# Layer 1's output projection as seven block products, woven into the value products

## The chip, the cores and the metric

The kernel runs on one core of one Trainium2 chip. The metric is the device time of one execution in microseconds; all arithmetic is 32-bit floating point. The engines of the core are named here as the profile names them: PE (TensorE, the matrix engine; PEld is its weight load), DVE (VectorE), ACT (ScalarE), POOL (GpSimd) and SP (SyncE, which only issues DMAs). Each works through its own queue in order and waits for the others by semaphores.

## The reference

Two layers, each of the form `x = x + layer(group_norm(x))`, over x of shape 1 x 128 x 256 x 256 (128 rows of 256 positions with 256 channels). Layer 0 is attention along each row with 8 heads, a bias computed from a second input z, and a gate. The change is in layer 1 alone, banded attention with 4 heads:

```python
qkv = x2 @ w_in.T + b_in                      # x2: rows of 256 positions, 256 channels
q, k, v = jnp.split(qkv, 3, axis=-1)          # 4 heads of 64 channels
scores = jnp.einsum('bhid,bhjd->bhij', q, k) / sqrt(64)
scores = jnp.where(abs(i - j) <= 16, scores, -inf)
attn = softmax(scores)
out = jnp.einsum('bhij,bhjd->bhid', attn, v)
y = out @ w_out.T + b_out                     # the output projection
```

## The kernel before

Layer 0 takes the first 1980 us or so of the execution, layer 1 the rest. In layer 1 the 128 rows are worked on in 64 pairs (`Pair1`, `NP = 64`), and the order of all instructions is written out by hand (`tc.manual_schedule()`): what the loop `for p in range(NP - 1)` calls is queued on each engine in just that order. In loop pass p three pairs are in work. `now` (pair p) gets its scores and its first row's value sums, `was` (pair p - 1) its second row's value sums and its output projection, and `nxt` (pair p + 1) its q, k and v. Pair p + 2 (`nn`) is centred, and for pair p + 3 (`n3`) the loads are issued and, at the end of the pass, the transpose `turn()` (DVE).

The steps that the prediction follows:

- `product(n, i)` and `join(n, i)` (lines 1955 and 1989; n = 0, 1, 2 for q, k, v): the projection of a pair by w_in is two rows times two halves of the channels, a 2 x 2 block product, computed with seven products instead of eight. Products 1, 6, 7, 4 go one after the other into one PSUM bank (x), and after each one ACT copies the running sum out (into `u`, after product 4 to its place); products 2, 5, 3 go into the bank y, and after each one a `join` on DVE adds the copy in `u` to it. So product 6 adds onto x only when ACT has copied it, and product 5 overwrites y only when DVE has read it. The sums of blocks that these products need are made once for the weights (`mix_weights`, `wst`) and once per pair for the data (`differences`, `dT`, four POOL instructions). For q and k (line 1978) a product is one matrix product of 256 columns, for v (line 1974) it is two of 128 columns. Every 32-bit matrix product is two MATMUL records in the profile, each with its weight load.
- `scores(r)` (line 2031): 64 records on tiles of 64 x 64; then four exponentials on ACT (`e`) and four multiplications by the band `bw` on POOL (line 2042).
- `apply(r)` (lines 2056 and 2064): the value products on tiles of 64 x 32 into `o_eo`, and the row sums of `e` into `su_eo`. Then ACT copies one half of each (`copy_sums`, `copy_odd`), DVE adds the other half (`join_sums` line 2081, `join_odd` line 2084), inverts the sums (`invert`, line 2087) and multiplies (`weigh`, line 2092): `oT[r]`, the transposed result of row r.
- `out_row(r)` / `out_block(r, b)` (line 2110): the output projection, for each row and each half of its 256 positions two products of 256 columns into `su_y`. `keep_row(r)` (line 2118, DVE) adds `xt` (the layer's input plus the output's bias, which `add_bias`, line 1933, adds on POOL) and writes `yo`; after row 1 SP stores it.
- `some_checks(n)` runs up to n entries of a list of range checks on DVE (lines 2143 to 2146), which feed a verdict at the end; for the last 8 pairs (`LATE`) there are more of them. What is left of the list is run after the loop.

`su_y` is one tile over two PSUM banks: the row sums lie in the first half of each bank, the output projection's result in the second halves.

Of the kernel before, what the change touches and what calls it, by code (L numbers as in the profile page):

```python
# [9 lines left out]
F32 = mybir.dt.float32  # L10
# [6 lines left out]
P = 128  # L17
# [756 lines left out]
def fast_kernel(  # L774
# [1057 lines left out]
    with tc.tile_pool(name="l1", bufs=2) as sb, tc.tile_pool(  # L1832
# [14 lines left out]
        for sign, base in ((1, 0), (-1, GE - 1)):  # L1847
# [2 lines left out]
                base=base, pattern=[[sign * P, KC], [-sign * GE, G]], channel_multiplier=sign,  # L1850
            )
        wst = sb.tile([P, 4, 3, P], F32, name="wst", bufs=1)

        def norm1():

# [29 lines left out]
        def mix_weights():  # L1885

            a = [[w_in[:, k].rearrange("p (n m c) -> p m n c", n=3, m=KC)[:, m] for k in range(KC)]
                 for m in range(KC)]
            s1, s2, s3, s4 = (wst[:, n] for n in range(4))
            nc.gpsimd.tensor_tensor(s1, a[1][0], a[1][1], ALU.add)  # L1890
            nc.gpsimd.tensor_tensor(s2, s1, a[0][0], ALU.subtract)
            nc.gpsimd.tensor_tensor(s3, a[0][0], a[1][0], ALU.subtract)
            nc.gpsimd.tensor_tensor(s4, a[0][1], s2, ALU.subtract)


        o_eo = [ps_o.tile([P, 2, I], F32, name=f"ps_o1_{n}", tag=f"o{n}") for n in range(2)]
        su_y = ps_o.tile([P, 2, 2, I], F32, name="ps_su_y1", tag="su")
        su_eo = [su_y[:, n, 0] for n in range(2)]

        class Pair1:  # L1900

# [52 lines left out]
            def product(self, n, i):  # L1954

                if len(self.ps) == n:
                    self.ps.append([mm1("ps_qk", n % 2) for _ in range(2)])
                    self.u.append(sm.tile([P, 3, I], F32, name="u1", tag=f"u{n}", bufs=2))
# [12 lines left out]
                if n == 2:  # L1971
                    for b in range(NB):
                        at = slice(b * P, (b + 1) * P)
                        nc.tensor.matmul(  # L1974
                            to[:, at], rhs[:, at], lhs, start=start and b == 0, stop=True, skip_group_check=True
                        )
                else:
                    nc.tensor.matmul(to, lhs, rhs, start=start, stop=True, skip_group_check=True)  # L1978
                u = self.u[n]
                if i in (2, 5, 3):  # L1980
                    return
                at = (1, 6, 7, 4).index(i)
                to = self.to[n](1, 0) if i == 4 else u[:, at]
                if n == 2:
                    nc.scalar.copy(to, x.rearrange("p (b c) -> p b c", b=NB) if i == 4 else x)
                else:
                    nc.scalar.activation(to, x, AF.Identity, bias=bin_c[:, n * KC + (at > 1) : n * KC + (at > 1) + 1])  # L1987
# [59 lines left out]
            def apply(self, r):  # L2047


                e = self.es[r]  # L2050
                gap = q0(2) - q0(0)
                for a in range(2):
                    for j in range(NK // 2):
                        for h in range(H1):
                            for k in (2 * j, 2 * j + 1):
                                nc.tensor.matmul(  # L2056
                                    o_eo[k % 2][h * DH : (h + 1) * DH, a, q0(k) : q0(k) + W],
                                    self.v[half(k), r, j, h * D1 + a * DH : h * D1 + (a + 1) * DH],
                                    e[half(k), h % 2, h // 2, j * W : (j + 1) * W], start=True, stop=True,
                                )  # L2060
                for h in range(H1):
                    for n in range(2):
                        two = su_y[h * DH : (h + 1) * DH, n].rearrange("p a i -> p (a i)")
# [39 lines left out]

            def out_block(self, r, b):
                if b == 0:
                    self.y = su_y[:, :, 1]
                    if self.p == NP - 1:
                        self.y = mm1("ps_y1", r).rearrange("p (b c) -> p b c", b=NB)
                for k in range(KC):
                    nc.tensor.matmul(  # L2110
                        self.y[:, b], self.oT[r][:, k, b * P : (b + 1) * P], w_out[:, k, :],
                        start=(k == 0), stop=(k == KC - 1),
                    )

            def keep_row(self, r):
                if r == 0:
                    self.yo = sb.tile([P, 2 * NB, C], F32, name="yo", tag="yo")
                nc.vector.tensor_tensor(
                    self.yo[:, r * NB : (r + 1) * NB, :], self.y,
                    self.xt[:, r * NB : (r + 1) * NB, :], ALU.add,  # L2120
                )
# [44 lines left out]
        with tc.manual_schedule():  # L2166
# [3 lines left out]
            mix_weights()  # L2170
            for k in range(KC):
                now.centre(k)
            for t in (*o_eo, su_y):
                nc.vector.memset(t, 0.0)
            nxt.turn()
            for m in range(KC):
# [8 lines left out]
            look_all(eb.rearrange("p h b i -> p (h b i)"), math.exp(-20.0))  # L2185
            n_eb = cols[0]

            was = Nobody()
            for p in range(NP - 1):
                nn = pair1(p + 2) if p == 0 else n3  # L2190
                n3 = pair1(p + 3)
# [10 lines left out]

                now.scores(0)
                now.scores(1)
                was.apply(1)
                nxt.begin_fast()
                was.copy_sums(1)
# [4 lines left out]
                for n in range(2):  # L2212
                    nxt.product(n, 2)
                    nxt.join(n, 2)
                was.invert(1)
                some_checks(p > 0)
                for i in (6, 5, 7):
                    for n in range(2):
                        nxt.product(n, i)
                for n in range(2):  # L2220
                    nxt.join(n, 5)
                was.join_odd(1)
                was.weigh(1)
                was.out_row(0)
                for n in range(2):
                    nxt.product(n, 4)
                    nxt.product(n, 3)
                    nxt.join(n, 3)
                fast = p < NP - 2
                if fast:  # L2230
                    nxt.product(2, 1)
                    nxt.product(2, 2)
                    nxt.join(2, 2)
                nn.centre(0)
                some_checks(2 if p > NP - LATE else 0)

                now.apply(0)
                now.copy_sums(0)
                if fast:
                    nxt.product(2, 6)  # L2240
                    nxt.product(2, 5)
                now.copy_odd(0)
                now.join_sums(0)
                was.out_block(1, 0)
                if fast:
                    nxt.product(2, 7)
                now.join_odd(0)
                some_checks(2 if p > NP - LATE else p > 0)
                was.out_block(1, 1)
                if fast:  # L2250
                    nxt.join(2, 5)
                was.keep_row(1)
                if fast:
                    nxt.product(2, 4)
                    nxt.product(2, 3)
                    nxt.join(2, 3)
                now.invert(0)
                now.weigh(0)
                nn.centre(1)
                nn.differences()  # L2260
                nn.add_bias()
                n3.turn()
# [3 lines left out]
                was, now, nxt = now, nxt, nn  # L2266

            now.scores(0)
            was.apply(1)
            was.copy_sums(1)  # L2270
            was.copy_odd(1)
# [104 lines left out]
```

## Time and profile before

| what | value |
|---|---|
| median of 3 runs | 3122.07 us (3119.59 to 3122.21) |
| the profiled execution | 3124.98 us |
| its span in the profile | 3123.2 us |
| mean granted PE clock | 0.987 |
| mean of L1974, 128-column products (first form) | 284 ns |
| mean of L1978, 256-column products (dT, wst) | 379 ns |
| mean of L2110, output projection in the loop | 386 ns |
| mean of L2092, `weigh` | 944 ns in the loop |
| mean of L1933, bias on POOL | 2383 ns |

A line L1974 is line 1974 of the kernel before. The mean of a matrix product is from its start to its modelled end; products overlap, so what one costs in a run of them is the distance from one start to the next, which is read from the chain or the timeline and is shorter. An engine's busy share is over the whole span, both layers together. "PE 100%" says that PE always has a product in flight, not that it is at its peak.

### The profile page before, as it was taken

Reading aid. Unit: us, or ns where it says so; the run is one execution under the profiler, and the core shown is the slowest. Engines: PE = TensorE matmul, PEld = TensorE weight load, DVE = VectorE, ACT = ScalarE, POOL = GpSimd, SP = SyncE. Lnnn points to the kernel's source line nnn. Section 1 sums busy time; section 2 is a strip of 40 time slices with the busy share of each in tenths; the row PEclk is TensorE's granted clock in tenths of the full one; section 3 lists DMA queues with packets and bytes.
Section 4 is the critical chain, followed back from the end, with each engine's and each line's share of the span. In section 5 each row is a group of like instructions: output and inputs, shape, how many; then the busy total and the mean of one; then the engine's idle time right before and its main releaser. Section 6 shows DMA issues by size and latency. Waiting matters only on the chain.

```text
span 3123.2 us, 80605 instructions
## 1 busy us (share of the span) xinstructions
PE 3020.6 (97%) x33642; PEld 2102.9 (67%) x33642; DVE 2397.7 (77%) x4010; ACT 1574.3 (50%) x2639; POOL 2267.1 (73%) x1636
## 2 busy tenths in 40 slices
PE   5689999999999999999999999899999999999998
PEld 4355555565555556555555655688888888888887
DVE  7986677777777777777777777688878777777788
ACT  3454544444444444444444444355555555555553
POOL 3469889888889989888998987454555555555553
PEclk9799999999999999999999999999999999999999
DMA  9952323323332332333233232443434343444431
GB/s 359 390 181 52 99 69 99 99 64 93 94 99 69 100 99 64 90 97 99 69 99 99 64 89 75 118 104 83 103 84 98 90 98 89 95 92 95 92 95 51
DMA packets 690774, 327.90 MB, mean 105 GB/s; under 512 B 538624, under 2 KB 639872, under 8 KB 689248
## 3 DMA queue, kind: packets, MB, share of 16 engines
q1 hardware_dynamic: 686000, 320.02, 38.3%
q8 instruction: 266, 4.36, 0.6%
q10 hardware_dynamic: 4400, 2.63, 0.3%
q14 instruction: 108, 0.88, 0.1%
HBM read 253.83 MB, written 68.74 MB: 103 GB/s over the span
## 4 chain that ended last, share of the span: by engine, by line
PE 92%; DMA 3%; DVE 3%; ACT 1%; POOL 1%; issue 1%; ACTq 0%; SPq 0%; POOLq 0%; DVEq 0%
PE ps_p L1364 21%; PE ps_qk L1978 12%; PE ps_sc L1401 9%; PE ps_ov L1436 8%; PE ps_y L1490 7%; PE ps_su_y L2110 7%; PE ps_qk L1974 7%; PE ps_v L1382 7%; PE ps_o L2056 4%; PE ps_su L1444 3%; PE ps_sc L2031 3%; PE ps_su_y L2064 2%; DMA xa<-in_x_dram 2%; DVE st L1199 1%; DMA zt<-in_z_dram 1%; PE ps_t L1143 1%
## 5 line engine op out<-in xcount | busy, mean ns | idle before, releaser
L1425 POOL TENSOR_TENSOR eboth<-e 128x512 f32<-128x512 f32 x512 | 743.4, 1473 | 178.3 <-PE ps_su L1444 98.4
L1421 DVE TENSOR_TENSOR e<-ps_sc,eb 128x1024 f32<-128x1024 f32 x384 | 458.5, 1222 | 292.3 <-ACT ps_sc L1413 292.2
L1413 ACT ACTIVATE ps_sc<-ps_sc 128x1024 f32<-128x1024 f32 x384 | 375.4, 1007 | 438.8 <-PE ps_sc L1401 313.1
L1401 PE MATMUL ps_sc<-qT,kT 32*128 32x256 f32 x4096 | 293.9, 400 | 0.0
L1941 POOL TENSOR_TENSOR dT<-xgT,dT 128x256 f32<-128x256 f32 x63 | 45.9, 728 | 313.7 <-ACT xgT L1927 313.7
L2042 POOL TENSOR_TENSOR e<-e,bw 128x384 f32<-128x384 f32 x256 | 248.1, 1000 | 10.7 <-ACT e L2040 10.7
L2110 PE MATMUL ps_su_y<-w_out,oT 128*128 128x256 f32 x1008 | 254.5, 386 | 0.9 <-DVE sums L2081 0.9
L1490 PEld LDWEIGHTS ps_y<-wo,oT 128*128 128x128 f32 x1024 | 195.5, 191 | 86.9 <-issue 44.2
L1401 PEld LDWEIGHTS ps_sc<-qT,kT 32*128 32x128 f32 x4096 | 185.5, 184 | 101.7 <-issue 91.3
L1490 PE MATMUL ps_y<-wo,oT 128*128 128x256 f32 x1024 | 244.7, 382 | 5.8 <-POOL oT L1480 5.8
L1436 PE MATMUL ps_ov<-e,v 128*32 128x256 f32 x4096 | 248.6, 383 | 0.0
L1364 PE MATMUL ps_p<-xnT,wq 128*128 128x512 f32 x512 | 247.6, 606 | 0.1
L1364 PE MATMUL ps_p<-xgT,wg 128*128 128x512 f32 x512 | 247.3, 605 | 0.0
L1382 PE MATMUL ps_v<-wv,xnT 128*128 128x256 f32 x1024 | 241.9, 379 | 0.0
L1364 PE MATMUL ps_p<-xnT,wk 128*128 128x512 f32 x512 | 240.7, 592 | 0.0
L1382 PEld LDWEIGHTS ps_v<-wv,xnT 128*128 128x128 f32 x1024 | 194.7, 190 | 53.8 <-issue 30.9
L2087 DVE RECIPROCAL rv<-sums 128x256 f32<-128x256 f32 x128 | 223.1, 1743 | 0.0
L1987 ACT ACTIVATE u<-ps_qk,bin_c 128x256 f32<-128x256 f32 x378 | 174.4, 475 | 95.0 <-PE ps_qk L1978 95.0
L2110 PEld LDWEIGHTS ps_su_y<-w_out,oT 128*128 128x128 f32 x1008 | 181.9, 190 | 22.2 <-DVE sums L2081 1.3
L1436 PEld LDWEIGHTS ps_ov<-e,v 128*32 128x32 f32 x4096 | 120.5, 110 | 109.0 <-issue 42.5
L1364 PEld LDWEIGHTS ps_p<-xnT,wk 128*128 128x128 f32 x512 | 97.3, 190 | 122.7 <-issue 122.5
L1940 POOL TENSOR_TENSOR dT<-xgT 128x256 f32<-128x256 f32 x63 | 46.0, 730 | 183.6 <-ACT xgT L1927 183.6
(234 smaller groups left out, 6608.5 us busy)
## 6 DMA issues: line engine op xcount, KB each, us to landing
xa<-in_x_dram SPq DMA_DIRECT2D x8, 4096.0 KB
xt<-in_x_dram SPq DMA_DIRECT2D x64, 512.0 KB
x<-xo SPq DMA_DIRECT2D x16, 2048.0 KB
xt<-x SPq DMA_DIRECT2D x64, 512.0 KB
rvb<-rsum SPq DMA_DIRECT2D x252, 128.0 KB
xs<-x SPq DMA_DIRECT2D x252, 128.0 KB
out_dram<-yo SPq DMA_DIRECT2D x63, 512.0 KB
xs<-in_x_dram SPq DMA_DIRECT2D x248, 128.0 KB
```

The source lines that it names most:

```text
L1364: nc.tensor.matmul(ps, w[:, k, m * P : (m + 1) * P], getattr(self, src)[:, k, :], start=(k == 0), stop=(k == KC - 1),)
L1382: nc.tensor.matmul(self.ps_v[:, b * C : (b + 1) * C], self.xnT[:, k, t * P : (t + 1) * P], wv[:, k, :], start=(k == 0), stop=(k == KC - 1),)
L1401: nc.tensor.matmul(self.pss[q // 2][:, q % 2, b, :], self.kT[rs, c, r * I + b * P : r * I + (b + 1) * P], self.qT[rs, c, r * I : (r + 1) * I],
L1413: nc.scalar.activation(self.pss[a], ps, AF.Exp)
L1421: nc.vector.tensor_tensor(es[a], pss[a], eb[:, h : h + 2], ALU.mult)
L1425: nc.gpsimd.tensor_tensor(t, es[a][:, :, 0, :], es[a][:, :, 1, :], ALU.add)
L1436: nc.tensor.matmul(ov[q * D0 : (q + 1) * D0, c, :], self.v[:, r, b, h * D0 : (h + 1) * D0], es[q // 2][:, q % 2, b, :], start=(b == 0), st ...
L1490: nc.tensor.matmul(self.ps_y[:, b * C : (b + 1) * C], self.oT[r][:, k, b * P : (b + 1) * P], wo[:, k, :], start=(k == 0), stop=(k == KC - 1),)
L1978: nc.tensor.matmul(to, lhs, rhs, start=start, stop=True, skip_group_check=True)
L2042: nc.gpsimd.tensor_tensor(e[:, q], e[:, q], bcast(bw.rearrange("p b w -> p (b w)"), 1, KC), ALU.mult)
L2087: nc.vector.reciprocal(self.rv[:, r, :], self.sums)
L2110: nc.tensor.matmul(self.y[:, b], self.oT[r][:, k, b * P : (b + 1) * P], w_out[:, k, :], start=(k == 0), stop=(k == KC - 1),)
```

## The change

The output projection of the pairs of loop passes 1 to 62 is computed by the same seven-product scheme over the pair's two rows: `out_product(i)` with 128-column products in place of `out_row`. The last two pairs, after the loop, keep the old form. `su_y` becomes two tiles, one per bank; the second half of bank 0 is x of the scheme, that of bank 1 is y. The sums of blocks of w_out are four POOL instructions in `mix_weights` (`wso`), those of the data four POOL instructions per pair (`row_sums`, `oS`). ACT copies after products 1, 6, 7, 4, DVE joins after 2, 5, 3. The input and bias are added by one POOL instruction per pair in the next pass (`keep_rows`), which also issues the store.

The order in the pass changes with it. `apply(0)` moves ahead of the last two products (4 and 3) of q and k; `join_odd(1)` ahead of the reciprocal; behind q's and k's last products come 14 steps in which the value products of `nxt` and the output products of `was` take turns. The transpose `turn()` of n3 moves into that run, and of the range checks in the late passes there are four entries instead of five. The buffer `u` has one copy instead of two. In `after`, the line numbers are some 7 higher up to `apply`; the new products are at line 2156, their copies at 2162 and 2164, the joins at 2169, `row_sums` at 2129 to 2132, `keep_rows` at 2172.

```diff
+        wso = sb.tile([P, 4, P], F32, name="wso", bufs=1)
...
+            a = [[w_out[:, k, m * P : (m + 1) * P] for k in range(KC)] for m in range(KC)]
+            s1, s2, s3, s4 = (wso[:, n] for n in range(4))
+            nc.gpsimd.tensor_tensor(s1, a[1][0], a[1][1], ALU.add)
+            nc.gpsimd.tensor_tensor(s2, s1, a[0][0], ALU.subtract)
+            nc.gpsimd.tensor_tensor(s3, a[0][0], a[1][0], ALU.subtract)
+            nc.gpsimd.tensor_tensor(s4, a[0][1], s2, ALU.subtract)
...
-        su_y = ps_o.tile([P, 2, 2, I], F32, name="ps_su_y1", tag="su")
-        su_eo = [su_y[:, n, 0] for n in range(2)]
+        su_y = [ps_o.tile([P, 2, I], F32, name=f"ps_su_y{n}", tag=f"su{n}") for n in range(2)]
+        su_eo = [t[:, 0] for t in su_y]
...
+            def row_sums(self):
+                self.oS = sb.tile([P, 4, I], F32, name="oS1", tag="oS", bufs=1)
+                b = [[self.oT[r][:, k, :] for r in range(2)] for k in range(KC)]
+                t1, t2, t3, t4 = (self.oS[:, n] for n in range(4))
+                nc.gpsimd.tensor_tensor(t1, b[0][1], b[0][0], ALU.subtract)
+                nc.gpsimd.tensor_tensor(t2, b[1][1], t1, ALU.subtract)
+                nc.gpsimd.tensor_tensor(t3, b[1][1], b[0][1], ALU.subtract)
+                nc.gpsimd.tensor_tensor(t4, b[1][0], t2, ALU.subtract)
...
+            def out_product(self, i):
...
+                x, y = (t[:, 1] for t in su_y)
+                w = lambda m, k: w_out[:, k, m * P : (m + 1) * P]
+                b = lambda k, r: self.oT[r][:, k, :]
+                to, rhs, lhs, start = {
+                    1: (x, w(0, 0), b(0, 0), True),
+                    2: (y, w(0, 1), b(1, 0), True),
+                    6: (x, wso[:, 1], self.oS[:, 1], False),
+                    5: (y, wso[:, 0], self.oS[:, 0], True),
+                    7: (x, wso[:, 2], self.oS[:, 2], False),
+                    4: (x, w(1, 1), self.oS[:, 3], False),
+                    3: (y, wso[:, 3], b(1, 1), False),
+                }[i]
+                for n in range(NB):
+                    at = slice(n * P, (n + 1) * P)
+                    nc.tensor.matmul(
+                        to[:, at], lhs[:, at], rhs, start=start and n == 0, stop=True, skip_group_check=True
+                    )
+                if i in (2, 5, 3):
+                    return
+                if i == 4:
+                    nc.scalar.copy(self.quarter(1, 0), x.rearrange("p (b c) -> p b c", b=NB))
+                else:
+                    nc.scalar.copy(self.uy[:, (1, 6, 7).index(i)], x)
...
+            def out_join(self, i):
+                m, r, at = {2: (0, 0, 0), 5: (1, 1, 2), 3: (0, 1, 1)}[i]
+                y, u = (t.rearrange("p (b c) -> p b c", b=NB) for t in (su_y[1][:, 1], self.uy[:, at]))
+                nc.vector.tensor_tensor(self.quarter(m, r), y, u, ALU.add)
...
+            def keep_rows(self):
+                nc.gpsimd.tensor_tensor(self.yo, self.yo, self.xt, ALU.add)
+                nc.sync.dma_start(rows(out, 2 * self.p, 2), self.yo)
...
                 now.scores(1)
+                old.keep_rows()
                 was.apply(1)
...
+                was.join_odd(1)
                 was.invert(1)
-                some_checks(p > 0)
                 for i in (6, 5, 7):
                     for n in range(2):
                         nxt.product(n, i)
+                nn.centre(0)
+
+                now.apply(0)
+                now.copy_sums(0)
                 for n in range(2):
                     nxt.join(n, 5)
-                was.join_odd(1)
                 was.weigh(1)
-                was.out_row(0)
+                was.row_sums()
+                some_checks(2 if p > NP - LATE else p > 0)
+                now.join_sums(0)
                 for n in range(2):
                     nxt.product(n, 4)
+                now.copy_odd(0)
+                for n in range(2):
                     nxt.product(n, 3)
                     nxt.join(n, 3)
+                now.join_odd(0)
                 fast = p < NP - 2
                 if fast:
                     nxt.product(2, 1)
                     nxt.product(2, 2)
                     nxt.join(2, 2)
...
+                nn.centre(1)
+                nn.differences()
+                nn.add_bias()
+                was.out_product(1)
+                was.out_product(2)
+                was.out_join(2)
                 if fast:
                     nxt.product(2, 6)
                     nxt.product(2, 5)
...
-                was.out_block(1, 0)
+                was.out_product(6)
                 if fast:
                     nxt.product(2, 7)
...
-                was.out_block(1, 1)
+                n3.turn()
+                was.out_product(5)
+                was.out_product(7)
                 if fast:
                     nxt.join(2, 5)
-                was.keep_row(1)
+                    nxt.product(2, 4)
+                some_checks(2 if p > NP - LATE else p > 0)
+                was.out_join(5)
                 if fast:
-                    nxt.product(2, 4)
                     nxt.product(2, 3)
                     nxt.join(2, 3)
+                was.out_product(4)
+                was.out_product(3)
+                was.out_join(3)
                 now.invert(0)
                 now.weigh(0)
```

More of the change, by code (lines that the diff above doesn't have):

```diff
@@ L1957, in product @@
                     self.ps.append([mm1("ps_qk", n % 2) for _ in range(2)])
-                    self.u.append(sm.tile([P, 3, I], F32, name="u1", tag=f"u{n}", bufs=2))
+                    self.u.append(sm.tile([P, 3, I], F32, name="u1", tag=f"u{n}", bufs=1))
                 x, y = (ps[:, :I] for ps in self.ps[n])
@@ L2062, in apply @@
                     for n in range(2):
-                        two = su_y[h * DH : (h + 1) * DH, n].rearrange("p a i -> p (a i)")
+                        two = su_y[n][h * DH : (h + 1) * DH].rearrange("p a i -> p (a i)")
                         nc.tensor.matmul(
@@ L2105, in out_block @@
                 if b == 0:
-                    self.y = su_y[:, :, 1]
+                    self.y = [t[:, 1] for t in su_y]
                     if self.p == NP - 1:
-                        self.y = mm1("ps_y1", r).rearrange("p (b c) -> p b c", b=NB)
+                        ps = mm1("ps_y1", r)
+                        self.y = [ps[:, n * C : (n + 1) * C] for n in range(NB)]
+                        self.whole = ps
                 for k in range(KC):
                     nc.tensor.matmul(
-                        self.y[:, b], self.oT[r][:, k, b * P : (b + 1) * P], w_out[:, k, :],
+                        self.y[b], self.oT[r][:, k, b * P : (b + 1) * P], w_out[:, k, :],
@@ new lines, in quarter @@
+            def quarter(self, m, r):
+                return self.yo[:, r * NB : (r + 1) * NB, m * P : (m + 1) * P]
+            def out_product(self, i):
+                if i == 1:
+                    self.yo = sb.tile([P, 2 * NB, C], F32, name="yo", tag="yo")
+                    self.uy = sm.tile([P, 3, I], F32, name="uy1", tag="uy", bufs=1)
+                x, y = (t[:, 1] for t in su_y)
[21 more added lines that the diff above has]
+                    nc.scalar.copy(self.uy[:, (1, 6, 7).index(i)], x)
@@ L2117, in keep_row @@
                     self.yo = sb.tile([P, 2 * NB, C], F32, name="yo", tag="yo")
[L2118 to L2121, printed above, removed]
+                if self.p == NP - 1:
+                    nc.vector.tensor_tensor(
+                        self.yo[:, r * NB : (r + 1) * NB, :], self.whole.rearrange("p (b c) -> p b c", b=NB),
+                        self.xt[:, r * NB : (r + 1) * NB, :], ALU.add,
+                    )
+                for t in range(r * NB, (r + 1) * NB if self.p < NP - 1 else 0):
+                    nc.vector.tensor_tensor(self.yo[:, t, :], self.y[t - r * NB], self.xt[:, t, :], ALU.add)
                 s0 = 2 * self.p
@@ L2172, in fast_kernel @@
                 now.centre(k)
-            for t in (*o_eo, su_y):
+            for t in (*o_eo, *su_y):
                 nc.vector.memset(t, 0.0)
@@ L2186, in fast_kernel @@
             n_eb = cols[0]
-            was = Nobody()
+            old = was = Nobody()
             for p in range(NP - 1):
@@ L2233, in fast_kernel @@
                     nxt.join(2, 2)
[L2234 to L2238, printed above, removed]
+                nn.centre(1)
[4 more added lines that the diff above has]
+                was.out_join(2)
                 if fast:
@@ L2241, in fast_kernel @@
                     nxt.product(2, 5)
-                now.copy_odd(0)
-                now.join_sums(0)
-                was.out_block(1, 0)
+                was.out_product(6)
                 if fast:
                     nxt.product(2, 7)
-                now.join_odd(0)
-                some_checks(2 if p > NP - LATE else p > 0)
-                was.out_block(1, 1)
+                n3.turn()
+                was.out_product(5)
+                was.out_product(7)
                 if fast:
                     nxt.join(2, 5)
-                was.keep_row(1)
+                    nxt.product(2, 4)
+                some_checks(2 if p > NP - LATE else p > 0)
+                was.out_join(5)
                 if fast:
-                    nxt.product(2, 4)
                     nxt.product(2, 3)
                     nxt.join(2, 3)
+                was.out_product(4)
+                was.out_product(3)
+                was.out_join(3)
                 now.invert(0)
                 now.weigh(0)
[L2259 to L2262, printed above, removed]
                 if p == NP // 2:
@@ L2265, in fast_kernel @@
                     below(n_eb, n_mask, 1e15)
-                was, now, nxt = now, nxt, nn
+                old, was, now, nxt = was, now, nxt, nn
             now.scores(0)
+            old.keep_rows()
             was.apply(1)
```

## The prediction

> **What bounds the kernel now.** The profiled execution took 3124.98 us, its span 3123.2 us; the median of the three timed runs is 3122.07. I carry the sum as a difference, so it applies to either. The page comes first: its busy table and the by-engine line of the chain that ended last.
>
> ```profile
> PE 3020.6 (97%) x33642; PEld 2102.9 (67%) x33642; DVE 2397.7 (77%) x4010; ACT 1574.3 (50%) x2639; POOL 2267.1 (73%) x1636
> PE 92%; DMA 3%; DVE 3%; ACT 1%; POOL 1%; issue 1%; ACTq 0%; SPq 0%; POOLq 0%; DVEq 0%
> ```
>
> Busy shares are averages over two layers, so the second view is the windows by stage. In layer 1's loop:
>
> ```profile
> 2600.00:2700.00 100.00, 100.00 (x1755) 86.88 (x1756) 76.47 (x114) 57.42 (x129) 55.02 (x52) 1.00 0.41 92
> ```
>
> The columns are TensorE, weight loads, VectorE, ScalarE, GpSimd, granted clock, DMA share, GB/s. TensorE is never idle, the clock is full, GpSimd is at 55%: only TensorE time per loop pass counts. The third view, the chain in order of time over one pass, gives it piece by piece (start, us, what):
>
> ```profile
> 2590.92 4.51 PE ps_qk L1978 x20
> 2595.43 1.73 PE ps_su_y L2110 x8
> 2597.16 1.73 PE ps_qk L1978 x8
> 2598.88 1.09 PE ps_qk L1974 x8
> ...
> 2601.26 1.09 PE ps_qk L1974 x8
> 2602.35 0.96 PE ps_su_y L2110 x4
> 2603.31 0.44 PE ps_qk L1974 x4
> 2603.76 0.87 PE ps_su_y L2110 x4
> 2604.62 0.89 PE ps_qk L1974 x8
> 2605.51 1.48 PE ps_sc L2031 x64
> ```
>
> The next pass's first product piece starts at 2608.28, so a pass is 17.36 us. Each matrix product is two records. A 256-column record costs 1.73/8 = 0.216 us, a 128-column one 0.89/8 = 0.111. Four pieces cost more than that: both long x8 pieces of L1974 (1.09, 0.20 over), the first row-1 block of L2110 (0.96, 0.10 over) and the first L1978 piece (4.51 against 20 x 0.216 = 4.33, 0.18 over). The fourth view, line L1974 by source, shows what such an excess is:
>
> ```profile
> L1974 PE MATMUL ps_qk<-wst,dT x744: 272/275/378, 2008.6 to 3075.4; 128*128 128x128 f32 x186
>   issue: 18.9, 62
> ```
>
> Minimum, median and maximum are 272, 275 and 378 ns: where a product's first weight load could not start ahead, about 0.10 us of it lies open. The 18.9 us of idle time before line L1974, 62 times 0.30, are the change from the small tiles of `apply` to full tiles, once per pass.
>
> **Part by part: TensorE.** Removed per pass: two `out_row`s, 16 records of 256 columns, 16 x 0.216 = 3.46 us. Added: seven products of two blocks, 28 records of 128 columns, 28 x 0.111 = 3.11. Difference -0.35. Three excesses move. (1) Value product 2 now waits for VectorE's q join 3, which the timeline shows ending at 2616.17 + 0.41 = 2616.58 while that product's group has been running since 2616.09: 0.10 wait and 0.10 open load. In the new order q's product 3, k's product 3 and value product 1 lie in front of it, and no `keep_row` on VectorE: -0.20 if the join is in time. (2) The 0.10 in front of the first row-1 block was its wait for `join_sums` (the block starts at 2602.19, VectorE's `sums` ends at 2601.70 + 0.42 = 2602.12; `su_y` is one tile); split in two and moved far behind that join: -0.10. (3) The 0.20 behind `apply(0)` stays, now before an L1978 product, 0.18 as behind `apply(1)`: -0.02. Together -0.67.
>
> A rule speaks against the 128-column form: the Trainium skill, "TensorE: Matmul & The Clock Gate", section "The mechanism" of Part 3, says that a weight load overlaps running matmuls only when its row group differs, and its section "LDWEIGHTS" gives columns / 1.2 GHz, 107 ns for 128. Were every load in the open, 28 x 0.107 against 16 x 0.107 would cost 1.28 us more a pass; with the -0.35 that is +0.93, a loss of 57 us over 61 passes. The row answers it: value products of this very shape, one load each, run at 0.111 us.
>
> **Does anything else become late?** The run of 18 steps alternates value and output products at 4 x 0.111 = 0.445 us each. On the x bank each next product waits for a ScalarE copy of the last (1, 6, 7, 4); on the y bank each waits for a VectorE join (2, 5, 3). The price of one hop is in the timeline:
>
> ```profile
> 2603.15 0.61 PE L1974 MATMUL ps_qk<-wst,dT 128*128 128x128 f32 x4
> 2603.80 0.37 ACT L1985 COPY u<-ps_qk 128x256 f32<-128x256 f32 x1 [0.99 <-PE ps_qk L1974]
> ```
>
> 0.61 from first start to last end, 0.04 to ScalarE, 0.37 copy, about 0.05 back, and the weight load wants to begin 0.11 ahead: 1.18 us from product to dependent product. Value 6 to 7, 7 to 4, output 6 to 7, 7 to 4 are each three products apart, 1.33: 0.15 to spare. Product 3 waits for a join that needs the copy of 7: 1.18 + 0.04 + 0.42 = 1.64 against four products, 1.78: 0.14 to spare, for values and outputs. Value 2: 0.59 (two 256-column records) + 0.04 + 0.42 + 0.05 + 0.11 = 1.21 against 0.43 + 0.43 + 0.445 = 1.31: 0.10. So seven of the fourteen products are tight by 0.10 to 0.15, the other seven have 0.3 or more. I allow 0.05 per pass (from 0, if all are in time, to 1.4, if all seven miss as value 2 does now at 0.20 each). Term: -0.62.
>
> ScalarE gains four copies of 0.37, 1.5 us on 57% of 17.4: 11.4 of 16.75. VectorE loses two `keep_row`s (0.68 each) and gains three joins (0.42): even, 13.3 (76.5%) of 16.75, and it is a queue in order: join 3 and both `out_join`s stand behind checks (0.3 to 0.7 us) in the first 25 passes or so (some 50 entries, two a pass), inside the 0.05.
>
> GpSimd carries the most:
>
> ```profile
> 2607.71 1.25 POOL L1943 TENSOR_TENSOR dT<-xgT,dT 128x256 f32<-128x256 f32 x1
> 2608.92 2.36 POOL L1933 TENSOR_TENSOR xt<-xt,bout_r 128x1024 f32<-128x1024 f32 x1
> 2611.24 3.86 POOL L2042 TENSOR_TENSOR e<-e,bw 128x384 f32<-128x384 f32 x4
> ```
>
> Now 3 x 0.73 + 1.25 + 2.36 + 3.86 = 9.7; `keep_rows` adds one 128x1024 op (2.36), `row_sums` four of 128x256 (2.9 to 3.4, as dT's): 15.0 to 15.5 of 16.75. Laid out from the start of `scores(0)`: masks 1.5 to 5.4, `keep_rows` to 7.8, then it waits for `weigh(1)` (VectorE: `sums` 3.5, two joins, `join_odd`, reciprocal 5.9 to 7.6, two joins, `weigh` 8.4 to 9.1), `row_sums` to 12.0 or 12.5, differences to 15.9, bias to 18.3 = 1.5 of the next pass. Its customers are later: `apply(0)` at 7.2 needs masks done at 3.5; output 6 at 13.0 needs the second sum, at 10.6; the next pass's product 6 at 4.6 needs differences done before that pass began. Cover 3.7, 2.4 and over 4 us; without it every us late would stand on the path. `weigh(1)` takes 1.25 where a mask runs beside it instead of 0.69 (2614.40, L2092); here it meets `keep_rows` or nothing, at most 0.8 by that line's maximum of 1.48, which the 2.4 covers.
>
> SyncE: the out DMA moves from the pass's end to behind `keep_rows` (7.8), the sums' DMA behind `weigh(1)` (9.1), the next loads behind both. Loads now start at 2605.81 and the transpose that reads their kind runs a pass later, about 20 us; 9.1 of one pass to 12.8 of the next (the transpose's new place) is the same 20. Nothing.
>
> Once only. First pass: `apply(0)` comes before values, at 1999.68 + 4.4 = 2004.1, but GpSimd's two bias ops (1999.40, 4.68) put the masks at 2004.1 to 2006.0: +1.9. Last loop pass: no value products to alternate with, the copy chain 3 x 1.18 + 2 x 0.445 = 4.4 against 3.56 now: +0.9. Tail: one check entry fewer per late pass puts eight more check instructions (0.28 to 0.42, some 2.4 us) before the last `keep_row`s, where VectorE idles 0.73: +1.7. The four `wso` ops lie in GpSimd's idle 5.4 us before 1995.43: nothing. Sum +4.5.
>
> 61 passes x -0.62 = -37.8; +4.5; -33.3 us. 3122.07 - 33.3 = 3088.8, for the profiled execution 3091.7.
>
> **Rivals.** *Part of it is lost:* one or two of the seven tight waits miss each pass, 0.20 each as value 2 misses now. -0.67 + 0.40 = -0.27, x 61 + 4.5 = -12: 3110 at two. For it: spare of 0.10 to 0.15 is smaller than the scatter VectorE's checks and `weigh` bring; passes of 17.6 to 18.4 us between score groups occur now. Against: the two joins and copies nearest in kind in today's value products do keep time.
> *Slower, by open weight loads:* the run turns into a chain of hops, product 4 and 7 of both kinds and both 3s late. Six x 0.20 = 1.2 - 0.67 = +0.53, x 61 + 4.5 = +37: 3159. It decides from the fourth late product per pass (three give 3122 + 0). Against it: a miss pushes the later products back and so gives the next hop its spare.
> *GpSimd becomes the bound* and holds the masks or sums: it needs its pass above 16.75, that is each op 8% dearer or one more collision of 0.5 on two ops, and above 17.4 to lose; 3.7 us of cover must go first. At 18.0: +0.6 x 61 = 3163.
> *Nothing changes:* three misses a pass.
>
> **How the numbers follow.** Forecast (up to half a miss) 0.60; part lost 0.25; nothing 0.03; slower by open loads 0.08; GpSimd 0.04. A measurement of this kernel tells about 0.2%, 6 us, from no change: faster 0.85, same 0.03, slower 0.12. The range's low end takes -0.76 a pass (the 128-column record before `apply` costs 0.09 more than others, and that place falls to a 256-column one): -46 + 4 = 3080, rounded to 3078; its high end is two misses, 3110.
>
> **What would show it.** Right: passes of 16.7 to 16.8 us between score groups; 28 records of the new line at 275 ns median, few at 378; GpSimd near 90%, TensorE 100%. Wrong: TensorE waits on ScalarE or VectorE inside the run, `apply(0)` waiting for GpSimd, passes above 17.

## The result: slower, and where it happens

The change takes 3168.47 us (median of 4 runs, 3165.91 to 3174.12) against 3122.01 for the kernel before on the same chip: ratio 1.0152, 95% interval 1.014 to 1.0164. The profiled execution took 3166.87 us, its span 3165.1. The page shows the kind of loss at once (busy table; the chain that ended last, by engine):

```profile
PE 3008.4 (95%) x34386; PEld 2100.6 (66%) x34386; DVE 2427.1 (77%) x4075; ACT 1656.9 (52%) x2887; POOL 2584.8 (82%) x1950
PE 85%; DVE 6%; DMA 4%; POOL 1%; ACT 1%; issue 1%; SPq 0%; POOLq 0%; ACTq 0%; DVEq 0%
```

TensorE's busy time fell by 12 us as records became cheaper, but it carries 85% of the chain where it carried 92%, and VectorE 6% where it carried 3%. The windows of layer 1's loop (columns as before: TensorE, weight loads, VectorE, ScalarE, GpSimd, granted clock, DMA share, GB/s) say that this is not so everywhere:

```profile
2200.00:2300.00 100.00, 91.14 (x1558) 79.93 (x1558) 80.17 (x122) 57.25 (x133) 74.65 (x72) 0.95 0.34 82
2600.00:2700.00 100.00, 98.64 (x1734) 86.75 (x1716) 76.00 (x126) 65.37 (x152) 85.92 (x84) 1.00 0.42 97
```

Early in the loop TensorE is 91% busy at a clock of 0.95; in the middle 98.6% at 1.00. A pass is measured from the start of its score group (L2038) to the start of the next pass's. So measured, the passes fall into two kinds. Passes 1 to 25 and 57 to 61, the ones in which `some_checks` still has entries of its list to issue, take 18.76 us or more; the others have a floor of 16.74. The span grew by 41.9 us: passes 1 to 25 gave +46.6, 26 to 56 gave -14.8, 57 to 61 +6.5, and start, first and last pass and tail +3.6.

In a pass without check entries the change is what it was forecast to be (chain in order of time, one pass from 2614.53 to 2631.27; its long pieces):

```profile
2617.30 4.51 PE ps_qk L1985 x20
...
2623.10 1.93 PE ps_qk L1985 x8
2625.02 0.89 PE ps_qk L1981 x8
2625.91 0.89 PE ps_su_y L2156 x8
2626.81 0.89 PE ps_qk L1981 x8
2627.70 0.45 PE ps_su_y L2156 x4
2628.15 0.45 PE ps_qk L1981 x4
2628.59 0.89 PE ps_su_y L2156 x8
2629.49 0.89 PE ps_qk L1981 x8
2630.38 0.89 PE ps_su_y L2156 x8
2631.27 1.48 PE ps_sc L2038 x64
```

Output products (L2156): 3.12 us, where the blocks took 1.73 + 0.96 + 0.87 = 3.56. Products of L1981: 3.12, where L1974 took 1.09 + 1.09 + 0.44 + 0.89 = 3.51. The piece behind `apply(0)` is now L1985's, 1.93 for 1.73. Sum: -0.44 - 0.39 + 0.20 = -0.63 per pass.

A pass with a check entry goes through the same steps until the last product but one. This is its end, from the timeline of all engines (start, us, engine, line; in brackets the idle time before it and who ended that):

```profile
2105.85 2.35 POOL L1940 TENSOR_TENSOR xt<-xt,bout_r 128x1024 f32<-128x1024 f32 x1
2105.97 2.38 DVE L2206 TENSOR_SCALAR above<-eb 128x256 f32<-128x256 f32 x1
...
2106.82 0.61 PE L2156 MATMUL ps_su_y<-w_out,oS 128*128 128x128 f32 x4
2107.80 0.37 ACT L2162 COPY yo<-ps_su_y 128x256 f32<-128x256 f32 x1 [0.86 <-PE ps_su_y L2156]
2108.39 0.42 DVE L2207 TENSOR_REDUCE ok<-above 128x1 f32<-128x256 f32 x1
2108.72 0.41 DVE L2169 TENSOR_TENSOR yo<-ps_su_y,uy 128x256 f32<-128x256 f32 x1
...
2109.19 0.52 PEld L2156 LDWEIGHTS ps_su_y<-wso,oT 128*128 128x128 f32 x4 [1.96 <-DVE yo L2169]
2109.19 0.71 PE L2156 MATMUL ps_su_y<-wso,oT 128*128 128x128 f32 x4 [1.77 <-DVE yo L2169]
```

Read it from the bottom. Output product 3 waits for `out_join(5)` (L2169), which has to read the y bank first. That join stands in VectorE's queue behind a check entry, and the entry's tensor_scalar (L2206), a 128x256 operation, takes 2.38 us. It starts 0.12 us after GpSimd's bias operation (L1940) and ends 0.15 us after it. The waits by pair, from 2060 to 3100 us, give the total (us, times, longest; the weight load and the matmul of the same product each have a row):

```profile
PEld ps_su_y L2156 <- DVE yo L2169: 51.5, 27, 2.0
PE ps_su_y L2156 <- DVE yo L2169: 46.4, 27, 1.8
```

The same instruction by source, in the kernel before and then in the changed kernel (minimum, median, maximum ns):

```profile
L2143 DVE TENSOR_SCALAR above<-eb x16: 282/284/285, 2027.4 to 2288.6; 128x256 f32<-128x256 f32 x16
```

```profile
L2206 DVE TENSOR_SCALAR above<-eb x16: 2314/2379/2394, 2028.0 to 2317.6; 128x256 f32<-128x256 f32 x16
```

Same operands, 284 ns then and 2379 now: it has moved from a place where the bias operation was not running to one where it is. Eight of the 25 passes are longer still, 20.2 us instead of 18.78. In these eight, after the idle time, the granted clock drops to 0.5 for 3.41 us, and the score group that follows is slow, 2.27 us instead of 1.55 in the one shown. Timeline of TensorE in one of them and in a pass without check entries, then a window inside the slow stretch of the first (columns as above):

```profile
2242.87 0.71 PE L2156 MATMUL ps_su_y<-wso,oT 128*128 128x128 f32 x4 [1.78 <-DVE yo L2169]
2243.51 2.27 PE L2038 MATMUL ps_sc<-qT,kT 64*64 64x96 f32 x64
...
2631.20 1.55 PE L2038 MATMUL ps_sc<-qT,kT 64*64 64x96 f32 x64
```

```profile
2244.20:2247.50 3.30, 3.30 (x124) 2.79 (x114) 2.41 (x2) 1.75 (x4) 2.40 (x3) 0.50 0.02 5
```

### The profile page after: what moved, and what is told of

Same layout as the page of the kernel before. It is cut to its first block, busy times and chain, and to the rows that moved or that the text cites. A ratio compares the mean times of both kernels' runs of the same rounds, so it can differ in the third digit from the quotient of the medians.

```text
span 3165.1 us, 83063 instructions
## 1 busy us (share of the span) xinstructions
PE 3008.4 (95%) x34386; PEld 2100.6 (66%) x34386; DVE 2427.1 (77%) x4075; ACT 1656.9 (52%) x2887; POOL 2584.8 (82%) x1950
## 4 chain that ended last, share of the span: by engine, by line
PE 85%; DVE 6%; DMA 4%; POOL 1%; ACT 1%; issue 1%; SPq 0%; POOLq 0%; ACTq 0%; DVEq 0%
PE ps_p L1364 21%; PE ps_qk L1985 12%; PE ps_sc L1401 9%; PE ps_ov L1436 8%; PE ps_y L1490 7%; PE ps_v L1382 7%; PE ps_qk L1981 5%; PE ps_su_y L2156 5%; PE ps_o L2063 4%; PE ps_su L1444 3%; PE ps_sc L2038 3%; DMA xa<-in_x_dram 2%; DVE above L2206 2%; PE ps_su_y L2071 2%; DVE st L1199 1%
## 5 line engine op out<-in xcount | busy, mean ns | idle before, releaser
L2049 POOL TENSOR_TENSOR e<-e,bw 128x384 f32<-128x384 f32 x256 | 276.7, 1110 | 135.8 <-ACT e L2047 135.8
L1116 POOL TENSOR_TENSOR zrs<-zrs,mhalf 128x32 f32<-128x32 f32 (+1 forms) x19 | 87.9, 4629 | 114.2 <-DVE zrs L1109 114.2
L1371 ACT ACTIVATE gT<-ps_p,bg_c 128x512 f32<-128x512 f32 x128 | 87.9, 687 | 175.1 <-PE ps_p L1364 175.1
L1985 PE MATMUL ps_qk<-dT,wst 128*128 128x256 f32 x756 | 173.5, 379 | 0.0
L2047 ACT ACTIVATE e<-ps_sc 128x384 f32<-128x384 f32 x256 | 105.8, 496 | 119.7 <-PE ps_sc L2038 119.0
```

The costliest lines, as they stand in the source:

```text
L2049: nc.gpsimd.tensor_tensor(e[:, q], e[:, q], bcast(bw.rearrange("p b w -> p (b w)"), 1, KC), ALU.mult)
```

## The experiments

Theory A: a tensor_scalar of VectorE cannot run while a GpSimd operation of this kind runs; it is held until that one instruction ends. Theory B, the rival: VectorE's queue is simply too full ahead of `out_join(5)`, with two more operations in it.

**The entries elsewhere.** Both entries of a pass ahead of `weigh(1)`, where GpSimd has no bias operation:

```
                 now.copy_sums(0)
                 ...
+                for _ in range(2):
+                    some_checks(2 if p > NP - LATE else p > 0)
                 was.weigh(1)
                 was.row_sums()
-                some_checks(2 if p > NP - LATE else p > 0)
...
-                some_checks(2 if p > NP - LATE else p > 0)
                 was.out_join(5)
```

> The changed kernel with both check entries of a pass moved ahead of weigh(1), where GpSimd stands idle because its next work (row_sums) waits for weigh(1). Theory A (VectorE's check instruction of line 2206 cannot run while GpSimd's bias instruction runs, takes 2.38 us instead of 0.28, and holds up the out_join behind it, for which output product 3 waits): line 2206 back at about 0.28 us, passes with checks 16.75 to 17.0 us instead of 18.8 to 20.2, the clock full; 3168 - 25 x 2.03 - 8 x 1.45 - 5 x 2.04 = 3096 us (3090 to 3102). Theory B (VectorE has no room for two check entries in a shorter pass, wherever they stand): passes stay at 18 us or more, 3150 to 3175 us.

Measured: 3104.16 us, ratio to before 0.9943 (0.9926 to 0.996). By source in this kernel:

```profile
L2206 DVE TENSOR_SCALAR above<-eb x16: 282/283/285, 2019.9 to 2276.2; 128x256 f32<-128x256 f32 x16
```

The duration is back at 283 ns, and the floor of passes 1 to 25 at 16.74; passes 57 to 61, with four entries each, still take 17.6 in the main. The time is 2 us above theory A's range of 3090 to 3102. Theory B had 3150 or more, since the same operations still stand in the same queue ahead of the same join.

**Another instruction in the same place.** The tensor_scalar replaced by a tensor_reduce that costs more by itself (0.41 us against 0.28), the threshold applied to the collected minima in `below`:

```
-                above = sm.tile([P, I], F32, name="above", tag="above", bufs=1)[:, : src.shape[1]]
-                nc.vector.tensor_scalar(above, src, lo, None, ALU.is_gt)
-                nc.vector.tensor_reduce(ok[:, 0, at : at + 1], above, AX.X, ALU.min)
+                again = sm.tile([P, 1], F32, name="again", tag="again", bufs=1)
+                nc.vector.tensor_reduce(again, src, AX.X, ALU.min)
+                nc.vector.tensor_reduce(ok[:, 0, at : at + 1], src, AX.X, ALU.min)
...
-        def below(start, stop, hi):
+        def below(start, stop, hi, lo):
+            nc.vector.tensor_scalar(ok[:, 0, start:stop], ok[:, 0, start:stop], lo, None, ALU.is_gt)
```

> The changed kernel, checks in their places; in the second kind of entry the comparison of line 2206 (0.28 us by itself) is replaced by a second reduction of the same data (0.36 to 0.42 us), the comparison with the limit is made once at the end on the results. So VectorE has no less to do. Theory A: nothing left that meets GpSimd, passes 16.75 to 17.0 us, 3096 us (3090 to 3105). Theory B: unchanged, passes 18.8 us, 3160 to 3172 us.

Measured: 3101.06 us, ratio 0.9934 (0.9917 to 0.995). VectorE has more work in the same order, and 67 us are gone. Theory B falls here.

**The same collision in the kernel before.** Its order of work is left alone, except that the entries go to the pass's end, where its bias operation runs:

```
-                some_checks(p > 0)
...
-                some_checks(2 if p > NP - LATE else 0)
...
-                some_checks(2 if p > NP - LATE else p > 0)
...
                 n3.turn()
+                some_checks(5 if p > NP - LATE else 2 * (p > 0))
```

> The kernel before, with its check entries (two per pass, five in the late passes) moved behind the transpose at the pass's end, where GpSimd runs the bias instruction of line 1933. Same instructions, same count. Theory A: line 2143 takes 1.5 to 2.0 us there, the joins of q and k behind it come late, 0.8 to 1.3 us more in some 30 passes: 3147 to 3162 us. Theory B: VectorE has as much room as before, 3122 us, within 4.

Measured: 3184.06 us, ratio 1.0196 (1.0179 to 1.0213). The direction is theory A's, the size is 22 us above the expected range. Passes 2 to 26 take 18.95 us instead of 17.37, with a tensor_scalar of 1.68: 1.58 more a pass, where 0.8 to 1.3 were expected, and 38 us in sum. Another 24 us come from passes 57 to 63, where I had put five entries in a row: TensorE waited up to 3.9 us there. The kernel before can be made slower than the changed one by nothing but the place of its check entries.

**How long is the hold?** The bias operation cut into four of 128x256:

```
-                nc.gpsimd.tensor_tensor(self.xt, self.xt, bcast(bout_r, 1, 2 * NB), ALU.add)
+                for t in range(2 * NB):
+                    nc.gpsimd.tensor_tensor(self.xt[:, t, :], self.xt[:, t, :], bout_r, ALU.add)
```

> The changed kernel with the bias instruction on GpSimd (128x1024, 2.36 us) cut into four of 128x256 (0.73 us each). Theory A with a hold for one instruction: line 2206 waits at most for one of the four, 0.3 to 1.0 us, TensorE waits 0.2 to 0.6 us before output product 3 in the passes with checks, 3102 to 3122 us. Theory A with a hold for as long as GpSimd has work queued: line 2206 at 2.4 us or more, 3168 us or more. Theory B: 3168 us.

Measured: 3114.10 us, ratio 0.9976 (0.9966 to 0.9985). By source in this kernel, the check's tensor_scalar and one bias piece:

```profile
L2207 DVE TENSOR_SCALAR above<-eb x16: 377/758/766, 2027.9 to 2287.3; 128x256 f32<-128x256 f32 x16
```

```profile
L1941 POOL TENSOR_TENSOR xt<-xt,bout_r x256: 715/728/791, 1996.4 to 3063.4; 128x256 f32<-128x256 f32 x128
```

The tensor_scalar now takes 0.76 us, and one GpSimd piece takes 0.73, although four of them follow each other without a gap. The hold ends with the instruction, not with GpSimd's queue. Passes 1 to 25 come to 17.16 in the main, passes 57 to 61 to 17.84.

**The half clock.** Three matmuls behind output product 4 fill most of TensorE's wait; their result is overwritten:

```
+            def keep_warm(self):
+                for _ in range(3):
+                    nc.tensor.matmul(
+                        su_y[0][:, 1], self.oT[1][:, 1, 0:P], w_out[:, 0, :],
+                        start=True, stop=True, skip_group_check=True,
+                    )
...
                 was.out_product(4)
+                if 0 < p <= 25:
+                    was.keep_warm()
                 was.out_product(3)
```

> The changed kernel with three matmuls of 128x256 f32 issued behind output product 4 of passes 1 to 25, into the accumulator that has just been copied out; their result is overwritten. They fill most of the 2 us in which TensorE waits for product 3. If the eight checked passes of 20.2 us come from the clock that is granted at half speed after that idle time: no half-clock stretch in passes 1 to 25, all checked passes at 18.8, 8 x 1.45 = 11.6 us less: 3155 to 3160. If the half clock is a by-product of something else in these passes: within 3 us of the changed kernel, 3165 to 3171.

Measured: 3151.44 us, ratio to before 1.0089 (1.0072 to 1.0106), 17.0 below the changed kernel and 4 below the forecast's range. The window that stood at 0.95 (windows view of this kernel):

```profile
2200.00:2300.00 100.00, 97.47 (x1730) 85.10 (x1731) 83.17 (x128) 58.56 (x137) 75.75 (x74) 1.00 0.35 82
```

No half-clock stretch is left in the loop, and no pass of 20.2. The two profiled spans differ by 14.3 us: 11.5 in passes 1 to 25, against 11.6 forecast for the clock, and 3.2 in passes 26 to 56, which run the same steps in both kernels. So the half clock was a consequence of the 2 us wait, and a sixth of the damage.

**What the change is worth without the collision.** As in the second experiment, but with a single reduction:

```
-                above = sm.tile([P, I], F32, name="above", tag="above", bufs=1)[:, : src.shape[1]]
-                nc.vector.tensor_scalar(above, src, lo, None, ALU.is_gt)
-                nc.vector.tensor_reduce(ok[:, 0, at : at + 1], above, AX.X, ALU.min)
+                nc.vector.tensor_reduce(ok[:, 0, at : at + 1], src, AX.X, ALU.min)
```

> The changed kernel with the low bound of a check taken by one tensor_reduce (minimum), the threshold applied once to the collected minima in below(). No tensor_scalar is left in passes 1 to 25 and 57 to 61, and one reduction less than in e2_reduce_twice. Theory A (a tensor_scalar of VectorE is held for the whole of a GpSimd instruction): 3096 to 3101, checked passes at 16.74 like the clean ones, passes 57 to 61 below the 17.0 of e2_reduce_twice; the third theory, for what is then still missing against the forecast (passes in which TensorE fetches three 16 KB blocks of instructions run 0.7 us longer, passes with two at 16.74): the same pattern of 3 longer passes in 7 stays. Theory B (VectorE too full): a few us below e2_reduce_twice, 3095 to 3098, with nothing left of the pattern.

Measured: 3098.99 us (3097.36 to 3102.7), ratio 0.9926 (0.991 to 0.9943). The reduction runs beside the bias operation at its own speed (timeline of this kernel, a pass with a check entry):

```profile
2078.13 2.37 POOL L1940 TENSOR_TENSOR xt<-xt,bout_r 128x1024 f32<-128x1024 f32 x1
2078.25 0.41 DVE L2205 TENSOR_REDUCE ok<-eb 128x1 f32<-128x256 f32 x1
```

To see whether the edit itself brought that, the same edit in the kernel before, and this kernel again beside it:

> The kernel before with the edit of e5_one_reduce (low bound by one minimum, no tensor_scalar in the passes). In before, the tensor_scalar of a check meets a GpSimd bias instruction only once, in the pass in which the collected bounds are closed, and else hides beside TensorE. Theory A: 3118 to 3123, within 0.1% of before, so that e5_one_reduce stays 0.7% below it and the gain belongs to the change. If the checks cost before's passes something too: below 3115.

> e5_one_reduce a second time, beside e9_before_one_reduce on one chip: 3097 to 3103; the ratio of the two is then the worth of the order and the seven products with the collision taken away: 0.990 to 0.995.

Measured: 3120.99 us for before with the edit, ratio 0.9996 (0.9986 to 1.0005); 3098.46 for the changed kernel with it, ratio 0.9921 (0.9904 to 0.9937). The edit is worth nothing to the kernel before. The gain of 0.7 to 0.8% belongs to the order and the products.

**What is missing still.** 3099 is 10 us above the forecast. In e5_one_reduce most passes take 16.74 us, but 22 of the 61 take 16.9 to 18.4, without any wait of TensorE's matmuls on another engine. The third theory: TensorE waits for its own instructions. The DMA queues of three passes in a row (42, 43, 44; each window begins and ends 3 us ahead of the pass; packets, MB, share), where pass 43 takes 18.41 us and its neighbours 16.74:

```profile
q8 instruction: 2, 0.03, 0.7%
...
q8 instruction: 3, 0.05, 1.0%
...
q8 instruction: 2, 0.03, 0.7%
```

The long pass is the one with three fetches of 16 KB, and its chain in order of time shows the idle time inside the values and sums of `apply`:

```profile
2729.19 0.21 issue
...
2735.87 0.78 issue
```

In e2_reduce_twice all 18 unchecked passes with two fetches took 16.74, the 13 with three 17.45 in the mean. In e5_one_reduce all 22 long passes have three fetches, but four more with three took 16.74. There are 2.43 fetches a pass now and 2.33 in the kernel before, whose passes have 24 fewer TensorE records (12 matmuls and their weight loads): some 240 instructions a fetch, an estimate from these numbers. The test adds instructions, so that the block ends move through the pass:

```
+            def small(self):
+                for _ in range(4):
+                    nc.tensor.matmul(
+                        su_y[0][0:32, 1, 0:32], self.oT[0][:, 0, 0:32], w_out[:, 0, 0:32],
+                        start=True, stop=True, skip_group_check=True,
+                    )
...
+                was.small()
                 was.out_product(1)
```

> e5_one_reduce with four tiny matmuls (32x32) ahead of output product 1 of each pass: 16 more TensorE instructions, 638 instead of 622, so that 2.5 blocks of 256 come to 640 and the places of the block ends in a pass move by only 2 instructions per pass, ahead 4 every second pass. Theory of the fetch: long passes come no longer 3 in 7 but every second one, odd passes from 1 to about 15 or 21, none from there to about 35, then even passes to the end; the other passes all at 16.74 plus the cost of the tiny matmuls (0.2 to 0.4); the time 3105 to 3125. If the longer passes have another cause (transfers, GpSimd, the check entries): 3 long passes in 7 at the same numbers as in e5_one_reduce, 3108 to 3122.

Measured: 3124.61 us, ratio 1.0005 (0.9995 to 1.0015). The floor of a pass rose to 17.31, by 0.57, more than the 0.2 to 0.4 I gave the tiny matmuls; that the time still lies in the range is luck. Long passes: the odd ones from 3 to 27 (17.4 to 18.0), none from 28 to 55, then 56 and 58. Nothing of 3 in 7 is left, as the theory had it, but the turns come at 27 instead of 15 to 21 and at 56 instead of about 35. The waits on "issue" in passes 1 to 26, then in 28 to 53:

```profile
PEld ps_o L2063 <- issue: 9.6, 29, 0.5
PEld ps_su_y L2071 <- issue: 3.3, 7, 0.6
PEld ps_qk L1985 <- issue: 3.2, 11, 0.3
```

```profile
PEld ps_o L2063 <- issue: 8.6, 26, 0.3
```

The 0.3 us of L2063, once a pass, stay; the rest vanishes in the second stretch. The number of fetches does not explain that: 13 of the passes 28 to 55 have three and take 17.31 like the others (passes 44 and 48, windows as above):

```profile
q8 instruction: 3, 0.05, 1.2%
...
q8 instruction: 3, 0.05, 1.2%
```

What goes with the long passes in these traces is the place of a fetch. In e5_one_reduce and here each long pass has one that starts within some 0.6 us of the start of its score group; of the other passes only four in e5_one_reduce and three here have one there. That speaks for TensorE's instruction stream as the cause, but that a fetch holds TensorE up is not shown.

**Order or products?** Four blocks as before, at the places of the products:

```
+            def out_copies(self, r):
...
+                nc.scalar.copy(self.yo[:, r * NB, :], self.y[0])
+                nc.vector.tensor_copy(self.yo[:, r * NB + 1, :], self.y[1])
...
-                was.row_sums()
...
-                was.out_product(1)
-                was.out_product(2)
-                was.out_join(2)
+                was.out_block(0, 0)
+                was.out_block(0, 1)
+                was.out_copies(0)
...
-                was.out_product(6)
...
-                was.out_product(5)
-                was.out_product(7)
+                was.out_block(1, 0)
...
-                was.out_join(5)
...
-                was.out_product(4)
-                was.out_product(3)
-                was.out_join(3)
+                was.out_block(1, 1)
+                was.out_copies(1)
```

> e5_one_reduce with the four output blocks of before (16 records of 128x256 in place of 28 of 128x128, no sums of GpSimd for them, no joins) at the places of the seven products, copied out by ScalarE and VectorE; the new order of the run stays. If the forecast's split holds (0.35 us of a pass from the records, 0.32 from the order): clean passes at 17.09, and with 598 instead of 622 TensorE instructions fewer passes with three fetches: 3108 to 3122. If the order alone carries the shorter pass: clean passes at 16.74, 3092 to 3100. If the products alone do: clean passes at 17.3 to 17.4, 3122 to 3132.

Measured: 3117.10 us, ratio 0.9982 (0.9972 to 0.9991); passes at 17.35, not 17.09. The time lies in the range of the forecast's split, but the pass is the 17.3 to 17.4 that "the products alone" had, so the time is right by luck. It does not separate the two cleanly, since leaving out products 6 and 7 made a new wait. The timeline (TensorE) and the waits of this kernel:

```profile
2509.28 1.89 PE L2119 MATMUL ps_su_y<-w_out,oT 128*128 128x256 f32 x8
2511.00 1.78 PE L1981 MATMUL ps_qk<-wst,dT 128*128 128x128 f32 x12
2512.62 1.03 PE L2119 MATMUL ps_su_y<-w_out,oT 128*128 128x256 f32 x4
```

```profile
PEld ps_qk L1981 <- ACT u L1992: 6.2, 30, 0.2
```

Eight block records take 2511.00 - 2509.28 = 1.72 us, 0.216 each: 0.35 a pass over the products, as forecast. The twelve records of value products 6, 5 and 7 take 1.62 where 1.34 was due: with no output product between them, value 7 follows 6 at 2 x 0.445 = 0.89 us, and the forecast's price for a hop over ScalarE was 1.18. That is 0.29 late, measured 0.28; with it taken off, the order alone would be worth some 0.3 us a pass, which is argued and not shown. No pass here is long, though every third has three fetches and in some one starts beside the score group (0.3 us behind it in pass 25); why, I did not test.

## Why the prediction was wrong

**The step that failed** is the sentence on VectorE: the joins "stand behind checks (0.3 to 0.7 us) in the first 25 passes or so ..., inside the 0.05". The price was that of the old place of the entries, 0.28 for the tensor_scalar, and the new place was not compared with what GpSimd does there. It had the same kind of price in hand: it put `weigh(1)` at 1.25 us beside a GpSimd mask instead of 0.69, and asked where the new order puts `weigh`, but not the checks. Measured: 2.38 us instead of 0.28, TensorE waiting some 2 us for it in 25 passes and most of that in five more. Taking it away brings 3168.47 to 3098.99, 69.5 us; of the spans' 69.1, 56.5 lie in passes 1 to 25, some 11.5 of those by the half clock, and 9.9 in passes 57 to 61. The trace of before showed the collision in a loop pass once, and I had seen the long pass without asking what made it long (source view of L2153 in the kernel before; its maximum overlaps the bias operation, in a pass of 18.44 us):

```profile
L2153 DVE TENSOR_SCALAR ok<-ok x3: 140/172/1857, 2573.6 to 3113.9; 128x16 f32<-128x16 f32 x1, 128x1 f32<-128x1 f32 x1, 128x28 f32<-128x28 f32 x1
```

The check's own line shows it too, in the tail: its 517 ns beside a mask of GpSimd, which ended 0.15 us before it (source view of L2143, kernel before):

```profile
L2143 DVE TENSOR_SCALAR above<-sums x12: 217/284/517, 2323.6 to 3103.8; 128x256 f32<-128x256 f32 x11, 128x128 f32<-128x128 f32 x1
```

**A second term was left out**: the long passes without a wait on another engine. Over passes 1 to 61 the time above the common pass is about 6 us in the kernel before and some 16.5 in e5_one_reduce and in its repeat. That is the 10 us by which these miss 3088.8. The forecast counted what an added record costs TensorE, but not that it also shifts the block ends of its instruction stream; what exactly makes these passes long stays open.

**What held.** -0.62 a pass: measured -0.63, with the record prices, the wait of value product 2 and that of the first row-1 block each at its forecast size. The open weight loads did not come: 28 records at 275 ns median, loads hidden. GpSimd is at 86%, and its own customers get their data in time. Once-only costs: first pass +1.3 (forecast +1.9), last +0.6 (+0.9), tail +1.9 (+1.7).

**The rivals.** None named this. "Part of it is lost" had the place (a join late for its product, with the checks ahead of it) but at 0.20 a miss. The GpSimd rival had the engine, but as a bound through its own results, not as something that stops another engine's instruction.

## What to carry to other kernels

When an instruction moves to another place in its queue, its duration has to be priced at the new place, beside what the other engines do at that time; look for the same operation's maximum, not its median, and ask what overlapped it. On a path with slack of 0.1 us, the VectorE operations to keep away from long GpSimd operations are the ones a trace has once shown stretched; a reduction in place of a compare, or GpSimd work cut in pieces, removes or shortens the hold. Look at the instruction stream of the bound engine too, though not by the count alone: with 16 instructions more a pass, e8_small_matmuls lost some 8 us above its floor where e5_one_reduce lost 16.5; its floor itself rose by more.

## What the runs showed of the hardware

- A tensor_scalar (128x256 f32, 0.28 us alone) that starts during a GpSimd tensor_tensor ends about 0.15 us after it: 2.38 us beside one of 2.35, 0.76 beside pieces of 0.73. A tensor_reduce of the same operand took 0.41 in the same place. The Trainium skill, "SBUF — State Buffer", section "Who interferes with whom", states this: the port pair that VectorE and GpSimd share is an exclusive lock for a whole instruction, tensor_scalar can take it under conditions and tensor_reduce never does. The runs agree.
- About 2 us of TensorE idle time were followed by half clock for 3.41 us in 8 of 25 passes. The Trainium skill, "TensorE: Matmul & The Clock Gate", section "🎯 Why this matters for your kernels", advises against gaps above about 3 us; here 2 us were enough, though not each time.
- In e2_reduce_twice unchecked passes with three 16 KB instruction fetches ran 0.7 us longer in the mean than passes with two (17.45 and 16.74 us); in e7_eight_blocks and in passes 28 to 55 of e8_small_matmuls they ran no longer. The cause is open.
